# Holding back the chains of small operations between the Gram matrix and the first gradient of an image

## The chip, the cores and the metric

The kernel runs on one core of one Trainium2 chip, in one launch. The metric is the device time of that launch in microseconds (us). The kernel before took 2804.1 us, the median of three runs (2804.09, 2804.1 and 2806.65).

## What is computed

A batch of 16 images with 64 channels of 128 x 128 points goes through four residual layers. Every layer first normalizes groups of two channels (`_gn`), and adds its result to its input:

```python
x = x + _L0_conv_ref(_gn(x), L0_conv_conv_w)   # Gram matrix over the points, times x, then a 1x1 convolution
x = x + _L1_conv_ref(_gn(x))                   # |Sobel x| + |Sobel y| of each channel
x = x + _L2_conv_ref(_gn(x), L2_conv_W, L2_conv_b)      # shifted 3x3 convolution
x = x + _L3_conv_ref(_gn(x), L3_conv_w_bin, L3_conv_w1x1, ...)  # 3x3, 1x1, batch norm over all images, clip
```

The first layer is linear in the image once the image's Gram matrix (64 x 64) and its channel sums are known:

```python
gram = jnp.einsum('bcn,bdn->bcd', xf, xf) / N
y = jnp.einsum('bcd,bdn->bcn', gram, xf)
out = jnp.einsum('oc,bchw->bohw', conv_w, y)
```

So the kernel needs the Gram sums of an image, makes from them one matrix per image that carries the whole first layer and the mean and deviation that the second layer's normalization needs, and applies it while it computes the gradients. The batch norm at the end needs sums over all the images.

## The kernel before

**Stages and steps.** Four stages work on different images at once: `Gram` (Gram sums on the matmul engine), `Front` (first layer as a matmul, then the Sobel gradients), `Layer2` and `Layer3`. An image has NS = 8 tiles, and one pass of the main loop over `step` moves each stage by one tile. `starts` says that image b reaches tile 0 of `Front` at step 15 + 8b, of `Layer2` at 25 + 8b and of `Layer3` at 35 + 8b. A step has four quarters, q = 0 to 3. All instructions are recorded through `InOrder`, so every engine executes them in the order in which the loop writes them; an engine whose next instruction waits does nothing else.

In what follows a step is named by the tile i that `Front` works on, i = (step - 15) mod 8. Eight steps make a period, in which one image passes each stage.

**Gram.** `pace` tells at which step an image's Gram work begins, and whether it goes at single or double speed. Images 1 to 6 go at double speed, four steps apart, and end at steps 16, 20, 24, 28, 32 and 36. Images 7 to 15 go at single speed and end at steps 47, 55, ... 111. At single speed the 128 matmuls per image come in blocks of 44, 42 and 42: in quarters 0 and 2 of a step with i = 7 and in quarter 0 of the step with i = 0 after it. At double speed all lie in one step. `pg` is their sum in PSUM; its pool `ps_g` has one buffer, which `pe` of `Front` uses too.

**The chain.** When the last block is issued, `gram_chain(b, pg)` is put into the list `chains`. It is a generator: `tick()` runs at the end of each quarter and lets each chain do one more piece, up to its next `yield`. One chain has 44 operations on VectorE, 19 matmuls (into the one PSUM tile `bank`) and two square roots on ScalarE, in 19 pieces, over four and a half steps. The pieces, by the names of what they write:

1. `gs`, the copy of `pg` out of PSUM
2. the matmuls `gd`; then `g`, `st`, `junk0`; the matmuls `pm`; then `me`, `nv`, `var` and the root `sd`
3. `r` (four operations) and `vv` (five); the matmuls `pr`; then `rw`; the matmul `pc`; then `cs`, `rc`
4. the matmuls `pq`; then `r2`, `wbd`, `ad`, `abd`; the matmuls `pd`; then `pp`, `av`; the matmuls `pk`
5. `bias`, `st1`, `t1`; the matmuls `pm`; then `me`, `nv`, `var`, `sd`; then `r` and `co1`

At the end `abd` (the matrix) and `co1` (the coefficients) are put into `lead[b]`. `Front` takes them at quarter 1 of its step -2, that is step 13 + 8b. The chain issues no DMA and nothing on GpSimd. The chains of the other two normalizations (`coefficients`) are in the same list.

**The order around it.** Within a quarter the loop writes `Layer3`, `Layer2`, `Front`, then `Gram`, then `tick()`. The instructions of `Front` that matter are: on VectorE `u<-xh`, the first of a step, with `e<-xh`; four operations on `u` and `e` in quarter 1; one each in quarters 2 and 3. On ScalarE, in quarter 2, two absolute values of `u` and `e` and then `xh<-po`, which empties the matmul's result `po` into `xh`. On the matmul engine `po<-x,abd` in quarters 1 and 3. `po` has one PSUM buffer, so the matmul in quarter 3 waits until ScalarE has emptied the one of quarter 1, and ScalarE has ahead of that the absolute values that wait for VectorE. `Layer2` issues `one<-v,wi` as its first matmul in quarter 2, and in the same tile of work `y` of `Layer3` is the first large VectorE operation of the quarter. `Layer2` also has GpSimd compute `edges` and correct `v`, for which VectorE's last `d<-v` of a step waits.

Of the kernel before, what the change touches and what calls it, by code (L numbers as in the profile page):

```python
# [10 lines left out]
F32 = mybir.dt.float32  # L11
# [4 lines left out]
B, C, H, W = 16, 64, 128, 128  # L16
P = 128
# [4 lines left out]
NS = HH // R  # L22
EARLY = 3
# [85 lines left out]
def tile_kernel(ctx: ExitStack, tc: tile.TileContext, x, cw_h, w2_t, b2, wbin_t, w1_t, b1, gamma, beta, consts, out):  # L109
# [11 lines left out]
    def k(name):  # L121
        return kc[:, AT[name][0]:AT[name][1]]
# [39 lines left out]
    stp = ctx.enter_context(tc.tile_pool(name="stp", bufs=2))  # L162
# [6 lines left out]
    def sv(name, n=1):  # L169
        return small.tile([P, n], F32, tag=name, name=name)  # L170
# [6 lines left out]
    def small_product(dst, wt, src):  # L177

        for o in (1 - last[0], last[0]):
            pe.matmul(dst[cols(o)], wt[:, cols(o)], src, start=True, stop=True)  # L180
        last[0] = o
# [5 lines left out]
    def sm(n, rows=P):  # L187
        if n > 8:
            return bank[0:rows, P:P + n]
        turn[0] = (turn[0] + 1) % 16  # L190
        return bank[0:rows, 8 * turn[0]:8 * turn[0] + n]
# [55 lines left out]
        nc.gpsimd.memset(twins[name], 0.0)  # L247


    chains = []  # L250

    def tick():
        for c in list(chains):
            if next(c, chains) is chains:
                chains.remove(c)
# [44 lines left out]

    def gram_chain(b, pg):

        gs = stp.tile([P, C + 1], F32, tag="gs", name=f"gs_{b}", bufs=1)
        dve.tensor_copy(gs, pg)
        if b > 1:
            yield
        gd = sm(C + 1)
        small_product(gd, k("same"), gs)
        yield
        g = stp.tile([P, C + 1], F32, tag="g", name=f"g_{b}", bufs=1)  # L310
        dve.tensor_scalar_mul(g, gd, 1.0 / HW)
        mu = g[:, C:C + 1]
        st = sv("st0", 2)
        dve.tensor_copy(st[:, 0:1], mu)
        junk0 = stp.tile([P, C], F32, tag="junk0", name=f"junk0_{b}", bufs=1)
        dve.scalar_tensor_tensor(
            junk0, g[:, 0:C], 1.0, k("Id"), op0=ALU.mult, op1=ALU.mult, accum_out=st[:, 1:2]
        )
        if b > 1:
            yield  # L320
        pm = sm(2)
        small_product(pm, k("gavg"), st)
        yield
        r, mean = yield from rstd(pm, GN_EPS)

        vv = sv("vv", 5)
        dve.tensor_scalar_mul(vv[:, 0:1], mu, -1.0)
        dve.tensor_sub(vv[:, 1:2], mu, mean)
        dve.tensor_copy(vv[:, 2:3], mu)
        dve.tensor_sub(vv[:, 3:4], mu, mean)  # L330
        dve.tensor_scalar_mul(vv[:, 4:5], mean, -1.0)
        if b > 1:
            yield
        pr = sm(2 * P, rows=2)
        pe.matmul(pr[:, 0:P], vv[:, 0:2], k("hsame"), start=True, stop=True)
        pe.matmul(pr[:, P:2 * P], vv[:, 2:4], k("hsame"), start=True, stop=True)
        yield
        rw = stp.tile([2, 2 * P], F32, tag="rw", name=f"rw_{b}", bufs=1)
        dve.tensor_copy(rw, pr)
        if b > 1:  # L340
            yield
        pc = sm(C)
        pe.matmul(pc, rw[:, 0:P], rw[:, P:P + C], start=True, stop=True)
        yield

        cs = stp.tile([P, 2, C], F32, tag="cs", name=f"cs_{b}", bufs=1)
        for s in range(2):
            dve.tensor_add(cs[:, s, :], pc, g[:, 0:C])
        rc = stp.tile([P, C], F32, tag="rc", name=f"rc_{b}", bufs=1)
        dve.tensor_scalar(rc, cwh, r, 0.5, op0=ALU.mult, op1=ALU.mult)  # L350
        csf = cs.rearrange("p s c -> p (s c)")
        if b > 1:
            yield
        pq = sm(C)
        small_product(pq, csf, rc)
        yield
        r2 = sv("r2")
        dve.tensor_mul(r2, r, r)
        for s in range(2):
            rows = slice(s * C, (s + 1) * C)  # L360
            dve.tensor_scalar_mul(wbd[rows, rows], pq[rows], r2[rows])
        ad = stp.tile([P, C], F32, tag="ad", name=f"ad_{b}", bufs=1)
        dve.scalar_tensor_tensor(ad, pq, r2, k("Id"), op0=ALU.mult, op1=ALU.add)
        abd = stp.tile([P, P], F32, tag="abd", name=f"abd_{b}", bufs=EARLY + 3)
        dve.tensor_add(abd, wbd, k("I"))
        if b > 1:
            yield
        pd = sm(C + 3)
        small_product(pd[:, 0:C], csf, ad)
        small_product(pd[:, C:C + 2], abd, vv[:, 2:4])  # L370
        small_product(pd[:, C + 2:C + 3], wbd, vv[:, 4:5])
        yield
        pp = stp.tile([P, 2, C], F32, tag="pp", name=f"pp_{b}", bufs=1)
        for s in range(2):
            dve.tensor_mul(pp[:, s, :], pd[:, 0:C], ad)
        av = sv("av", 3)
        dve.tensor_copy(av, pd[:, C:C + 3])
        if b > 1:
            yield
        pk = sm(1)  # L380
        small_product(pk, pp.rearrange("p s c -> p (s c)"), k("q"))
        yield
        bias = sv("bias")
        dve.tensor_copy(bias, av[:, 2:3])
        st1 = sv("st1", 2)
        dve.tensor_add(st1[:, 0:1], av[:, 0:1], bias)
        t = sv("t1")
        dve.scalar_tensor_tensor(t, av[:, 1:2], av[:, 1:2], pk, op0=ALU.mult, op1=ALU.subtract)
        dve.scalar_tensor_tensor(
            st1[:, 1:2], st1[:, 0:1], st1[:, 0:1], t, op0=ALU.mult, op1=ALU.subtract  # L390
        )
        if b > 1:
            yield
        pm = sm(2)
        small_product(pm, k("gavg"), st1)
        yield
        r, mean = yield from rstd(pm, GN_EPS)

        co = stp.tile([P, 4], F32, tag="co1", name=f"co1_{b}", bufs=EARLY + 3)
        dve.tensor_copy(co[:, 0:1], r)  # L400
        dve.tensor_sub(co[:, 1:2], bias, mean)
        dve.tensor_mul(co[:, 1:2], co[:, 1:2], r)
        dve.reciprocal(co[:, 2:3], r)
        dve.tensor_copy(co[:, 3:4], mean)
        lead[b] = abd, co

    class Gram:
# [5 lines left out]
        def at(self, i, q):  # L413
# [29 lines left out]
            if n == 6:  # L443
                chains.append(gram_chain(b, self.pg))
# [416 lines left out]
    starts = ((Layer3, 35), (Layer2, 25), (Front, 15))  # L861
    live = {}

    def run(stage, b, i, q):
        if 0 <= b < B and stage.first <= i <= stage.last:
            if (stage, b) not in live:
                live[stage, b] = stage(b)
            live[stage, b].at(i, q)
# [27 lines left out]
    def slices(t, n):  # L896
        room.extend(t[:, j * N:(j + 1) * N] for j in range(n))
# [11 lines left out]
            fetched[0] += 1  # L909

    for step in range(steps):
        for q in range(4):
            for b in range(B):

                i = step - starts[2][1] - NS * b
                if 0 <= i < NS and q in (0, 2):
                    live[Front, b].sobel(i, f"first of {q}")
                if q == 3:
                    run(Layer2, b, step - starts[1][1] - NS * b, "first of 3")
            for stage, at in starts:  # L920
                for b in range(B):
                    run(stage, b, step - at - NS * b, q)
            if q == 3:
                for b in range(B):
                    run(Layer2, b, step - starts[1][1] - NS * b, "last of 3")
            for b in range(B):
                at, n = pace[b]
                for m in range(n):
                    v = 4 * n * (step - at) + n * q + m
                    run(Gram, b, v // 4, v % 4)  # L930
            tick()

            if step == last_one - NS and q == 0:
                slices(xw.rearrange("p w c t -> p (w c t)"), 8)
                slices(xh.rearrange("p a j w -> p (a j w)"), 3)
                rest(xin, "x", [R, W], 2)
                rest(xin, "xr", [C // 8, W], 3)
                rest(work, "u", [R + 1, W + 2], 2)
                rest(work, "e", [R, W + 2], 1)
            if step == last_one and q == 0:  # L940
                rest(ring, "v2", [(R + 1) * W + 2], 3)
                for t in (diffs["d2"], twins["d2"]):
                    slices(t.rearrange("p n j w -> p (n j w)"), 1)
            if step >= last_one and q == 2:

                n = 3 if step == last_one else 1 if step < last_one + NS - 2 else 0
                rest(ring, "x3", [2, CP, W], NS + 2, n)

            if step >= last_one - NS and q == 3 and len(room) > 1:
                fetch()  # L950
# [82 lines left out]
```

## Time and profile before

| what | us |
|---|---|
| median of the three runs | 2804.1 |
| the profiled execution, its own time | 2800.37 |
| its span, from first to last instruction | 2798.6 |
| matmul engine (PE) busy | 2222.1 |
| VectorE (DVE) busy | 2201.4 |
| ScalarE (ACT) busy | 2120.1 |
| GpSimd (POOL) busy | 859.5 |
| the last matmuls, those of the batch norm's sums | 2349.13 |

Times inside a profile count from the start of its span. The part from 2349 us on is the last pass, which reads two arrays, adds them and writes the output; the change does not touch it. Before it, the main loop goes through three stretches: up to about 329 us (step 34) the pipeline fills; from there to about 1760 us (step 118) all stages work, Gram sums among them; from there to step 155 there are no Gram sums left to make.

A view of windows gives, for each stretch of time, how long each engine was busy in it and (in brackets) with how many instructions. The busy time of the matmul engine has modelled ends and says little on whether it waited; the starts of its instructions in the timeline do.

### The profile page before, as it was taken

To read this page: it belongs to the slowest core of one execution; us is meant where nothing else is said; L and a number is where in the kernel's file an instruction comes from. 1 tells how busy PE (TensorE), PEld (TensorE's weight loads), DVE (VectorE), ACT (ScalarE), POOL (GpSimd) and SP (SyncE) were. 2 spreads that over 40 slices of the span, in tenths; PEclk is the share of its full clock that TensorE was granted. 3 is DMA by queue.
4 is the path that set the end of the run, shared out by engine and by line. 5 is a ranking of instruction groups with operands and counts; after the bars stand their busy time and mean duration, and the time that the engine had idled before them with its cause. 6 is when DMAs were issued, how large, how long until landed. Compare 5 with 4: busy or idle time off the path is not lost. (4 is left out here: it accounts for less than half of the span.)

```text
span 2798.6 us, 46299 instructions
## 1 busy us (share of the span) xinstructions
PE 2222.1 (79%) x14772; PEld 1088.8 (39%) x14772; DVE 2201.4 (79%) x3758; ACT 2120.1 (76%) x3171; POOL 859.5 (31%) x1326
## 2 busy tenths in 40 slices
PE   4568899999999999999999999999999995000000
PEld 2323444444444545353534353566666641000000
DVE  3999999898989898989898989999997435333332
ACT  4667779888888888888888888998997667333332
POOL 1035433343434343434343434444444310000000
PEclk7679999999999999999999999999999998555555
DMA  6789878888888888888888777888877767999999
GB/s 168 196 221 233 237 198 237 218 232 212 230 215 221 222 220 219 222 216 227 221 219 227 214 184 197 209 204 214 209 207 187 218 192 273 420 420 420 420 420 387
DMA packets 688880, 685.95 MB, mean 245 GB/s; under 512 B 61744, under 2 KB 590144, under 8 KB 688640
## 3 DMA queue, kind: packets, MB, share of 16 engines
q1 hardware_dynamic: 662656, 614.42, 73.9%
q0 software_dynamic: 24576, 68.12, 10.0%
q8 instruction: 119, 1.95, 0.3%
q14 instruction: 121, 0.99, 0.1%
q10 hardware_dynamic: 1408, 0.46, 0.1%
HBM read 346.23 MB, written 268.44 MB: 220 GB/s over the span
## 5 line engine op out<-in xcount | busy, mean ns | idle before, releaser
L73 PE MATMUL two<-d,w 128*64 128x508 f32 (+2 forms) x2560 | 898.2, 586 | 0.0
L73 PE MATMUL two<-d,wi 128*64 128x508 f32 (+3 forms) x1536 | 626.6, 576 | 0.0
L73 POOL DMA_DIRECT2D qd<-d x512 | 269.8, 529 | 882.2 <-issue 330.0
L73 PE MATMUL two<-qd,pk 128*64 128x512 f32 (+1 forms) x1024 | 518.5, 587 | 1.6 <-DMA qd<-d 1.1
L73 POOL TENSOR_SCALAR edges<-v,co 64x8 f32<-64x8 f32 x512 | 335.2, 655 | 352.5 <-ACT v L73 244.4
L73 PE MATMUL po<-x,abd 128*64 128x512 f32 x1024 | 386.2, 631 | 60.4 <-ACT xh L73 60.4
L73 PEld LDWEIGHTS two<-d,w 128*64 128x64 f32 x2560 | 297.9, 136 | 288.7 <-issue 221.2
L73 PE MATMUL one<-v,w 128*64 128x508 f32 (+2 forms) x1600 | 409.0, 578 | 0.0
L73 PE MATMUL one<-v,wi 128*64 128x508 f32 (+3 forms) x1536 | 407.4, 590 | 0.0
L73 DVE TENSOR_TENSOR d<-v 128x512 f32<-128x512 f32 (+1 forms) x512 | 346.1, 679 | 44.4 <-POOL v L73 17.1
L73 ACT COPY qd<-d 64x512 f32<-64x512 f32 x512 | 315.2, 616 | 21.0 <-DVE d L73 14.5
L73 ACT ACTIVATE xh<-po,co 128x128 f32<-128x128 f32 (+1 forms) x480 | 275.3, 621 | 51.0 <-PE po L73 48.7
L73 DVE SCALAR_TENSOR_TENSOR e<-e 128x1032 f32<-128x1032 f32 (+1 forms) x256 | 313.2, 1223 | 0.0
L73 DVE SCALAR_TENSOR_TENSOR y<-two,c 128x1024 f32<-128x1024 f32 x128 | 156.1, 1219 | 125.6 <-ACT v L73 72.4
L73 PEld LDWEIGHTS two<-d,wi 128*64 128x64 f32 x1536 | 196.1, 135 | 143.2 <-issue 107.7
L73 POOL TENSOR_SCALAR v<-v,kc 128x9 f32<-128x9 f32 x256 | 238.4, 944 | 11.9
L73 ACT ACTIVATE v<-x,co 128x512 f32<-128x512 f32 (+2 forms) x368 | 234.9, 704 | 0.0
L73 PEld LDWEIGHTS one<-v,w 128*64 128x64 f32 x1600 | 163.3, 137 | 177.4 <-issue 130.0
L73 PEld LDWEIGHTS one<-v,wi 128*64 128x64 f32 x1536 | 156.0, 138 | 162.6 <-issue 126.4
L73 ACT ACTIVATE u<-u 128x1024 f32<-128x1024 f32 x128 | 135.4, 1058 | 90.3 <-DVE u L73 89.9
L73 DVE SCALAR_TENSOR_TENSOR u<-xh 128x1170 f32<-128x1170 f32 x128 | 175.7, 1372 | 12.2 <-ACT xh L73 9.8
L73 PEld LDWEIGHTS po<-x,abd 128*64 128x64 f32 x1024 | 111.0, 140 | 175.4 <-ACT xh L73 92.3
(154 smaller groups left out, 3442.4 us busy)
## 6 DMA issues: line engine op xcount, KB each, us to landing
xr<-in_x SPq DMA_DIRECT2D x128, 512.0 KB, 6.7
x<-in_x SPq DMA_DIRECT2D x256, 256.0 KB, 4.0
x_d<-u SPq DMA_DIRECT2D x512, 128.0 KB, 3.6
y_d<-y SPq DMA_DIRECT2D x512, 128.0 KB, 4.0
x_d<-x SPq DMA_DIRECT2D x496, 128.0 KB, 2.5
qd<-d POOLq DMA_DIRECT2D x256, 130.0 KB, 3.0
qd<-d POOLq DMA_DIRECT2D x256, 129.8 KB, 3.6
v<-x_d SPq DMA_DIRECT2D x448, 72.1 KB, 3.0
```

Of the source, the lines that this page charges most:

```text
L73: return self.tc.keep_in_program_order(call(*args, **kwargs))
```

## The change

`gs` is copied as before, one tick after the Gram matmuls. The chain then yields until the step counter has reached 15 + 8b - 9, that is, until nine steps ahead of tile 0 of the image's `Front`, a step with i = 7. It goes on from there with the same pieces in the same order. `gs` gets five buffers in place of one. `abd` gets three in place of six, and `co1` four in place of six. Images 0 and 1 get their Gram sums later than that step and don't wait.

```diff
+    now = [0]
     chains = []
...
     def gram_chain(b, pg):
 
-        gs = stp.tile([P, C + 1], F32, tag="gs", name=f"gs_{b}", bufs=1)
+        gs = stp.tile([P, C + 1], F32, tag="gs", name=f"gs_{b}", bufs=EARLY + 2)
         dve.tensor_copy(gs, pg)
         if b > 1:
             yield
+
+        while now[0] < starts[2][1] + NS * b - 9:
+            yield
         gd = sm(C + 1)
...
-        abd = stp.tile([P, P], F32, tag="abd", name=f"abd_{b}", bufs=EARLY + 3)
+        abd = stp.tile([P, P], F32, tag="abd", name=f"abd_{b}", bufs=3)
...
-        co = stp.tile([P, 4], F32, tag="co1", name=f"co1_{b}", bufs=EARLY + 3)
+        co = stp.tile([P, 4], F32, tag="co1", name=f"co1_{b}", bufs=4)
...
     for step in range(steps):
+        now[0] = step
         for q in range(4):
```

The pieces after `gs` move as follows:

| image | step of the copy, before and after | steps of the other pieces before | after |
|---|---|---|---|
| 1 | 16 | 17 to 21 | the same |
| 2 | 20 | 21 to 25 | 22 to 26 |
| 3 | 24 | 25 to 29 | 30 to 34 |
| 4 | 28 | 29 to 33 | 38 to 42 |
| 5 | 32 | 33 to 37 | 46 to 50 |
| 6 | 36 | 37 to 41 | 54 to 58 |
| 7 | 47 | 47 to 52 | 62 to 66 |
| ... | | | |
| 14 | 103 | 103 to 108 | 118 to 122 |
| 15 | 111 | 111 to 116 | 126 to 130 |

## The prediction

> **What bounds the kernel now.** I read the page first, then busy times step by step (windows cut where VectorE starts `u<-xh`), then timelines. The page, with busy tenths in 40 slices of 70 us:
>
> ```profile
> PE 2222.1 (79%) x14772; PEld 1088.8 (39%) x14772; DVE 2201.4 (79%) x3758; ACT 2120.1 (76%) x3171; POOL 859.5 (31%) x1326
> ...
> PE   4568899999999999999999999999999995000000
> ...
> DVE  3999999898989898989898989999997435333332
> ```
>
> Two engines are near full, and VectorE fills first. The windows of one period in the middle (i = 7, 0, 1, ... 6; columns: length, then busy time of PE, weight loads, DVE, ACT, POOL with counts), and of one period after the last Gram sums:
>
> ```profile
> 923.37:939.34 15.97, 15.97 (x175) 8.44 (x173) 14.65 (x20) 15.69 (x25) 4.45 (x10) 1.00 0.99 242
> 939.34:961.47 22.13, 22.13 (x233) 12.12 (x231) 16.35 (x35) 15.50 (x26) 4.96 (x12) 1.00 0.72 193
> 961.47:977.97 16.50, 16.50 (x125) 9.49 (x123) 16.15 (x37) 15.95 (x26) 5.79 (x11) 1.00 0.92 235
> 977.97:995.71 17.74, 17.74 (x89) 6.55 (x87) 16.94 (x31) 16.29 (x26) 8.50 (x11) 1.00 0.88 236
> 995.71:1013.28 17.57, 17.57 (x98) 6.29 (x96) 17.09 (x36) 15.17 (x24) 4.68 (x9) 1.00 0.80 216
> 1013.28:1029.33 16.05, 16.05 (x84) 6.79 (x82) 15.64 (x28) 14.96 (x24) 6.16 (x12) 1.00 0.84 234
> 1029.33:1045.24 15.91, 14.89 (x69) 8.06 (x67) 15.59 (x28) 13.72 (x23) 8.42 (x11) 1.00 0.82 208
> ...
> sum 136.77, PE 135.75 PEld 62.70 DVE 126.96 ACT 122.05 POOL 50.38; mean PE 16.97 PEld 7.84 DVE 15.87 ACT 15.26 POOL 6.30
> ```
>
> ```profile
> 1901.03:1915.54 14.51, 14.51 (x98) 9.86 (x96) 14.37 (x20) 12.42 (x20) 6.63 (x8) 1.00 0.83 222
> ...
> sum 124.15, PE 124.15 PEld 79.95 DVE 120.59 ACT 113.39 POOL 58.31; mean PE 15.52 PEld 9.99 DVE 15.07 ACT 14.17 POOL 7.29
> ```
>
> In the middle VectorE has 9.8 us to spare per period, 7.1 of them in i = 7 and 0, where the Gram blocks hold up PE. In i = 1 to 5, where the chain is, VectorE is full and PE catches up with it, until PE has to wait in i = 5 (timeline of PE):
>
> ```profile
> 904.35 1.01 PE L73 MATMUL two<-d,wi 128*64 128x508 f32 x2
> 906.37 1.08 PE L73 MATMUL po<-x,abd 128*64 128x512 f32 x4 [1.01 <-ACT xh L73]
> ```
>
> That is the loop over VectorE's `u`, ScalarE's absolute values and `xh`, and PE's `po`. Starts 1.60 us apart where 0.43 is the spacing of such matmuls: 1.2 us lost. The PE timeline has no other such gap in a period, only about 0.3 us in small ones: 1.5 us per period lost, the rest is PE's own work. VectorE's waits in i = 0:
>
> ```profile
> 943.82 0.38 DVE L73 TENSOR_TENSOR two<-two,edges 128x8 f32<-128x8 f32 x2 [1.96 <-PE two L73]
> ...
> 954.23 1.22 DVE L73 SCALAR_TENSOR_TENSOR y<-two,c 128x1024 f32<-128x1024 f32 x1 [3.44 <-ACT junk L73]
> ```
>
> The second is really for PE: the last matmul of its `two` starts at 953.55 and takes 0.59. The reader is to see that 5.4 us of VectorE in i = 0 are free. While the pipeline fills, VectorE bounds (steps 25 to 34):
>
> ```profile
> sum 154.42, PE 127.26 PEld 55.97 DVE 143.96 ACT 107.89 POOL 82.33; mean PE 12.73 PEld 5.60 DVE 14.40 ACT 10.79 POOL 8.23
> ```
>
> [...]
>
> **The change, part by part.** Nothing is removed: 16 chains stay, with all operations, and no DMA, SyncE or GpSimd instruction is in them. Order on the engines changes, and 14 chains move. One chain on VectorE, start to start in the period shown: `g` to `junk0` 0.47, `me` to `var` 0.54, `r` and `vv` 1.03, `rw` 0.34, `cs` and `rc` 0.42, `r2` to `abd` 1.28, `pp` and `av` 0.35, `bias` to `st1` 0.78, `me` to `var` 0.52, `r` to `co1` 1.28: 7.0 us. On PE: the time from one step's first `one<-v,wi` to the next one's is 15.6, 17.0, 16.1, 15.9, 15.7 us with a chain (i = 0 to 4) and 15.4, 15.9, 15.5, 15.4, 15.4 without; less 0.3 of waits, 2.4 us.
>
> *Filling (to step 34).* By the table of steps, pieces leave steps 21 to 34 worth 10.4 us of VectorE: chain 4 (7.0), chain 5 up to `rw` and about 1 net of chain 2 moved later. Not all comes back: in steps 27 to 29, with no chain left, VectorE's last `d` would come at 11 to 12 us into the step, while GpSimd's correction of `v` ends at 12.4 to 13.3 now. I take off 4 us for that, and 1 for waiting longer on the Gram block ahead of `gs` in step 28 (0.96 us already). Gain 5 us; bounds 2 and 9.
>
> *PE's work in the full part.* Chains 6 to 15 and 0.6 of chain 5 lie after step 34 now; then chains 4 to 15 do. 1.4 more at 2.4: a loss of 3.4 us, bounds 2 and 5.
>
> *Nine periods with Gram blocks (chains 5 to 13, in place of 7 to 15).* Pieces now fall on i = 7 (1.01 us), 0 (1.37), 1 (1.70), 2 (1.13), 3 (1.80). The first 2.0 are free in VectorE's waits. There `var` waits for `pm`, which stands behind the second Gram block: PE gets there about 1.8 us after VectorE, and VectorE stands still, with the next step's `u<-xh` behind it. The 5.4 us of i = 0 cover that too; if not, that is the third rival. The rest I follow with one number, D: the start of PE's first `one<-v,wi` in a step less the start of VectorE's `u<-xh` in it. It grows by PE's time for the step and shrinks by VectorE's. Now, by the timelines, D is 8.3, 8.8, 7.2, 5.5, 5.1 at i = 1 to 5 (18.76 less 13.28 at i = 4), and in the last periods without chains 7.8 to 8.1, 9.2, 8.3, 7.4, 8.2. `po` waits once D falls under a floor, read from `xh`'s end after `u<-xh`: about 5.7 at i = 4 and 5, and 7.5 at i = 3 with a piece of 0.52 ahead of it. At i = 1, D becomes 8.3 - 0.3 (`rw`) + 1.2 (`pr`, `pc`, `pq` are on PE there by then) = 9.2. Then 9.2 + 16.4 - 16.2 = 9.4; + 15.6 - 17.5 = 7.5, just at its floor; + 15.4 - 18.1 = 4.8 at i = 4, 0.9 under its floor; after that D recovers. Lost 0.9 per period in place of 1.5: gain 0.6 times 9, 5.5 us. An error of 1 us in D is 1 us per period: bounds from a gain of 13 to a loss of 3 within one model.
>
> *The end (chains 14 and 15).* They now run where no Gram block gives VectorE a rest. D starts at about 7.9 at i = 7; with PE's and VectorE's times of that stretch and the pieces added it goes 8.7, 6.8, 7.0, 5.1, so PE loses 2.4 at i = 3 and 0.9 at i = 4: 3.3 per chain, 6.6 us, bounds 3 and 9. Before, PE waits 1.3 us for `qd` once at 1742 us, with D down from the last chain; half of it goes: 0.7.
>
> *Buffers.* Five `gs` hold three waiting sums at most (images 4 to 6 at step 36), `abd` and `co1` are in use for two images at a time. No wait; nothing. `lead[b]` is ready at step 10 + 8b and taken at 13 + 8b: no wait of `Front`.
>
> Sum: -5 + 3.4 - 5.5 + 6.6 - 0.7 = -1.2 us. Against the profiled execution (2800.37 us; span 2798.6 and 1.8 around it) that is 2799; its own time lies 3.7 under the median shown, 2804.1, to which I apply the difference and get 2803.
>
> **Rivals.** (1) *It cancels* (forecast): what filling and the Gram steps give, the end takes. 2797 to 2809.
>
> (2) *Faster.* The free time in i = 7 and 0 ends PE's waits altogether: nine times 1.5 is 13.5; filling gives 8, the end costs 4: -8 + 3.4 - 13.5 + 4 - 0.7 = -15, 2789. For it: VectorE's 7.1 us there are over three times the pieces' 2.4. Against: the other 4.6 us fall on three steps in place of 6.2 on five, and one, i = 3, already carries the small operations of `Layer3`'s coefficients.
>
> (3) *Slower.* Place: i = 3 and 4 in every period. If D at i = 1 is not 9.2 but at the 7 of the end stretch, because the wait for `pm` is not covered, PE loses 3.3 per period as there: 1.8 more than now, nine times 16. With the other terms, -5 + 3.4 + 16 + 6.6 - 0.7 = +20, 2824. It decides from D under 8.6 at i = 1, where 1.5 is lost as now. For it: i = 3 gets 1.80 us on top of a full step. Against: in i = 0 it is PE that is late, by 14.8 in D.
>
> (4) *It doesn't do what it says* for images 0 and 1, by the table; for the others the order of instructions shows the move.
>
> **How the numbers follow.** Within 0.2%, 5.6 us, is what a measurement can't tell from no change. Cancels 0.40, faster 0.27, slower 0.33, which includes couplings of the three full engines that one number D doesn't follow. The single terms' bounds together (about 3 to 9 each, of different sign) give 2793 to 2812 around the forecast alone; 2788 to 2819 takes in the faster case and the lower part of the slower one.
>
> **What would show it.** Right: steps 21 to 34 shorter by about 5 us in all; in the middle, a period of 136.2 against 136.8, VectorE's busy time in i = 7 and 0 up by 2.4 at the same lengths, the wait on `po` at i = 4 and not 5; periods from 1745 us on longer by 3 plus PE's 2.4. Wrong: i = 0 longer than 22.1 by a microsecond or more, `po` waiting over 2 us at i = 3, or no wait at all.

## The result: slower by 0.6%, and the profile after

| | before | after |
|---|---|---|
| median, us | 2804.1 | 2820.74 |
| the profiled execution, its own time | 2800.37 | 2819.42 |
| its span | 2798.6 | 2817.6 |

The ratio is 1.0058, with a 95% interval of 1.0043 to 1.0073. The forecast was 2803, its range 2788 to 2819. The page of the changed kernel shows little (busy time with its share and instructions, then busy tenths in 40 slices of the span):

```profile
PE 2235.1 (79%) x14772; PEld 1021.4 (36%) x14772; DVE 2202.8 (78%) x3758; ACT 2121.7 (75%) x3171; POOL 832.1 (30%) x1326
...
PE   3567899999999999999999999999999995000000
...
DVE  3998989898989898989898989999997435333332
```

The instructions are as many as before, and VectorE's busy time grew by 1.4 us. So for VectorE nearly all of the 19.05 us by which the span grew are waits. The windows of the middle period that answers to the one shown of before (shown are i = 7, 0, 2, 3 and the sum; columns: length, then busy time of PE, weight loads, DVE, ACT, POOL with counts, then PE's granted clock, the DMA engines' busy share and GB/s):

```profile
927.83:947.16 19.33, 19.33 (x244) 11.10 (x242) 15.68 (x27) 16.35 (x27) 5.11 (x12) 1.00 0.98 232
947.16:968.07 20.91, 20.91 (x174) 9.11 (x172) 17.60 (x45) 16.32 (x26) 5.05 (x10) 1.00 0.70 183
...
984.26:1002.99 18.73, 18.73 (x111) 10.65 (x108) 17.15 (x34) 16.10 (x26) 7.54 (x12) 1.00 0.85 236
1002.99:1020.82 17.83, 17.33 (x80) 7.36 (x78) 17.27 (x39) 15.12 (x25) 4.20 (x8) 1.00 0.81 219
...
sum 137.46, PE 136.76 PEld 60.52 DVE 127.18 ACT 122.52 POOL 49.62; mean PE 17.10 PEld 7.56 DVE 15.90 ACT 15.31 POOL 6.20
```

The period is 0.7 us longer than the one shown of before, not 0.6 shorter (over the nine periods it is 0.4 on average). Look at i = 2, which begins at 984.26: 18.73 us long with 17.15 us of VectorE's work in it. In before VectorE had 0.8 us without work in this step; here it has 1.6. The view that finds the cause sums up what VectorE waited for over the whole kernel (us in total, times, the longest). Before:

```profile
DVE me L73 <- PE bank L73: 0.9, 2, 0.5
```

After:

```profile
DVE me L73 <- PE bank L73: 37.0, 24, 3.5
```

`me` is the copy of a small product's result out of PSUM. It waited twice before, and 24 times now. Two of the 24 are the old ones; nine are in i = 7, about 1.97 us each, where the prediction had one of about 1.8 and called it covered. The other thirteen are all in i = 2, from step 33 to step 129, and nobody expected them. One of them, in the timelines of VectorE and then of PE, in i = 2 of the period above:

```profile
998.21 0.21 DVE L73 SCALAR_TENSOR_TENSOR t<-av,bank 128x1 f32<-128x1 f32 x1
...
1002.33 0.16 DVE L73 COPY me<-bank 128x2 f32<-128x2 f32 x1 [1.24 <-PE bank L73]
```

```profile
998.48 0.28 PE L73 MATMUL bank<-s,kc 128*64 128x2 f32 x4
...
1001.22 0.23 PE L73 MATMUL bank<-st,kc 128*64 128x2 f32 x2
...
1002.06 0.23 PE L73 MATMUL bank<-st,kc 128*64 128x2 f32 x2
```

Two lists of small operations meet here. `t` and `bank<-st` (the second `pm`) belong to the Gram chain. `bank<-s` and this `me` belong to the coefficients of the third normalization, the one that `Layer2` ends with. `me` reads what `bank<-s` wrote at 998.48, yet it starts only after the chain's last `bank<-st`, at 1002.06 and 3.6 us later, of which it needs nothing. And in the stretch without Gram blocks, PE's timeline and VectorE's:

```profile
1816.63 0.28 PE L73 MATMUL bank<-s,kc 128*64 128x2 f32 x4 [1.75 <-DVE t L73]
```

```profile
1816.37 0.21 DVE L73 SCALAR_TENSOR_TENSOR t<-av,bank 128x1 f32<-128x1 f32 x1
...
1820.48 0.16 DVE L73 COPY me<-bank 128x2 f32<-128x2 f32 x1 [1.24 <-PE bank L73]
```

Here PE stands 1.75 us and starts nothing else, before a matmul for which `t` gives nothing either; `s`, which it does read, was ready at 1813.2. What they share is a place. All small products of the chains are written into one PSUM bank, the narrow ones at columns that take turns:

```python
    bank = ps_sm.tile([P, 512], F32, name="bank")
    ...
    def sm(n, rows=P):
        if n > 8:
            return bank[0:rows, P:P + n]
        turn[0] = (turn[0] + 1) % 16
        return bank[0:rows, 8 * turn[0]:8 * turn[0] + n]
```

`t` reads other columns than `bank<-s` writes, and `bank<-s` waits for it all the same. The trace shows the two waits, 1.24 us of VectorE and 1.75 us of PE; by what rule they are ordered it doesn't show. The prediction counted on no wait of this kind.

So in these two waits a read and a product within `bank` keep the order in which the program writes them down, though their columns differ. In quarter 2 of i = 2 the changed program has the chain's `bias` to `t`, then the coefficients' `bank<-s`. In quarter 3 it has the chain's `bank<-st`, then the coefficients' `me`. They are out of step: in each quarter one list's VectorE piece stands beside the other's product, and whoever is behind pays. `me` has to wait for a product written down just ahead of it, with no quarter of lead. In the kernel before both had their products in quarter 2 (`pc`, which is `bank<-rw`, and `bank<-s`) and their VectorE pieces in quarter 3 (`cs` and `me`), and nobody waits (PE, then VectorE, in i = 2):

```profile
991.99 0.43 PE L73 MATMUL bank<-rw 2*128 2x64 f32 x2
992.35 0.28 PE L73 MATMUL bank<-s,kc 128*64 128x2 f32 x4
```

```profile
994.64 0.35 DVE L73 TENSOR_TENSOR cs<-bank,g 128x64 f32<-128x64 f32 x2
...
995.06 0.15 DVE L73 COPY me<-bank 128x2 f32<-128x2 f32 x1
```

Where the spans differ, from the times at which VectorE starts the steps (differences to the profile of before, us; the column e1 is the first experiment below):

| stretch | predicted | after | e1 |
|---|---|---|---|
| up to step 15 | 0 | +1.2 | +1.6 |
| steps 15 to 34 | -5 | +2.8 | -0.5 |
| steps 34 to 46 | -1.4 | -0.7 | -2.3 |
| steps 46 to 118, nine periods with Gram blocks | -5.5 | +4.0 | -5.1 |
| steps 118 to 134, chains 14 and 15 | +10.7 | +13.2 | +10.9 |
| from there on | 0 | -1.5 | -1.2 |
| sum | -1.2 | +19.0 | +3.4 |

(The PE term of the prediction is laid out here by its chains: two more after step 118, 0.6 fewer in steps 34 to 46; the -0.7 is in the end. The profiled execution of before lies 3.7 us under its median, so a column that sums to +3.4 is about level with the medians of before. The first two rows differ from execution to execution: over steps 15 to 34 the profiles of four kernels with the same order of instructions there, before, e2, e4 and e7, take 251.8 to 258.6 us. In the other rows before and e2 differ by 0.4 us at most.) While the pipeline fills, the same meeting is in step 33, and the wait is longer there (PE, then VectorE):

```profile
308.68 0.28 PE L73 MATMUL bank<-s,kc 128*64 128x2 f32 x4 [1.97 <-DVE t L73]
```

```profile
314.23 0.16 DVE L73 COPY me<-bank 128x2 f32<-128x2 f32 x1 [3.54 <-PE bank L73]
```

The windows from the start of `bank<-s` to that of `me`, in step 33 and in step 73 of the middle, show what is different:

```profile
308.68:314.23 5.55, 5.51 (x22) 1.87 (x22) 2.01 (x4) 1.91 (x3) 1.08 (x2) 0.69 1.01 249
998.48:1002.33 3.85, 3.85 (x27) 1.69 (x28) 2.61 (x6) 2.58 (x4) 0.94 (x2) 1.00 0.59 161
```

PE's granted clock was 0.69 in the one (0.50 from 310 to 313 us) and 1.00 in the other, and 5.55 times 0.69 is 3.83, about the length of the other. So by this estimate 1.7 us of the 3.54 come from the lower clock. The other 0.6 by which the wait is longer than 1.24 come from VectorE, which is at `me` that much sooner. The clock fell just after PE had stood 1.97 us for `t`; that the standing was the reason isn't shown.

### The profile page after: what moved, and what is told of

Read it like the earlier page. It is cut to its first block, busy times and chain, and to the rows that moved or that the text cites. A ratio compares the mean times of both kernels' runs of the same rounds, so it can differ in the third digit from the quotient of the medians.

```text
span 2817.6 us, 46286 instructions
## 1 busy us (share of the span) xinstructions
PE 2235.1 (79%) x14772; PEld 1021.4 (36%) x14772; DVE 2202.8 (78%) x3758; ACT 2121.7 (75%) x3171; POOL 832.1 (30%) x1326
## 5 line engine op out<-in xcount | busy, mean ns | idle before, releaser
L73 PE MATMUL two<-d,w 128*64 128x508 f32 (+2 forms) x2560 | 869.3, 587 | 0.0
L73 PE MATMUL two<-d,wi 128*64 128x508 f32 (+3 forms) x1536 | 608.4, 579 | 0.0
L73 PEld LDWEIGHTS two<-d,w 128*64 128x64 f32 x2560 | 281.1, 136 | 311.9 <-issue 258.3
L73 PE MATMUL po<-x,abd 128*64 128x512 f32 x1024 | 340.7, 632 | 64.8 <-ACT xh L73 64.0
L73 DVE TENSOR_TENSOR d<-v 128x512 f32<-128x512 f32 (+1 forms) x512 | 346.9, 680 | 47.4 <-issue 16.4
L73 PE MATMUL one<-v,w 128*64 128x508 f32 (+2 forms) x1600 | 383.8, 579 | 0.0
L73 PE MATMUL one<-v,wi 128*64 128x508 f32 (+3 forms) x1536 | 369.5, 587 | 0.0
L73 POOL TENSOR_SCALAR v<-v,kc 128x9 f32<-128x9 f32 x256 | 220.2, 873 | 11.9
L73 PEld LDWEIGHTS one<-v,w 128*64 128x64 f32 x1600 | 138.5, 136 | 183.9 <-issue 149.9
L73 PEld LDWEIGHTS one<-v,wi 128*64 128x64 f32 x1536 | 137.4, 137 | 164.2 <-issue 135.8
L73 ACT ACTIVATE v<-v,co 128x1154 f32<-128x1154 f32 x128 | 172.0, 1344 | 15.6 <-DMA v<-x_d 8.1
```

Of the source, the lines that this page charges most:

```text
L73: return self.tc.keep_in_program_order(call(*args, **kwargs))
```

## The experiments

Theory 1 says that the meeting in one bank is the loss. Theory 2, its rival, says that the place is: the chain's 7 us of VectorE lie where there is no rest, and a wait there takes what would be lost anyway. Every kernel here computes the whole result.

### e1: another bank for one of the two

```diff
-    def coefficients(st, put, back=None):
+    def coefficients(st, put, back=None, place=None):
...
-        pm = sm(2)
+        pm = sm(2) if place is None else place()
         small_product(pm, k("gmean"), s2)
...
-                    chains.append(coefficients(self.st, lambda co: coefs3.update({b: co})))
+                    chains.append(coefficients(
+                        self.st, lambda co: coefs3.update({b: co}),
+                        place=lambda: ps_g.tile([P, CP, W], F32, tag="g", name=f"ps3_{b}")[:, 0, 0:2],
+                    ))
```

> The changed kernel, with one thing different: the matmul of the sums for the third normalization (Layer2's coefficients, in the step with i = 2) writes into the PSUM bank that the Gram sums use, which is free then, and not into the bank of the chain's small products. Same instructions, same order. Theory 1 (the shared bank): in i = 2 the chain and the coefficients take turns in one bank, so PE's product waits for VectorE's `t1`, and VectorE's `me` waits for PE's `pm`; this costs the 1.24 us of VectorE seen in every i = 2, and PE's 1.9 us twice after 1745 us. Then these waits are gone, D at i = 3 goes from 6.2 to above 7, the period falls from 137.5 to about 136.5, step 33 gives back 3, and the whole is 10 to 18 us faster than the changed kernel: 2803 to 2811. Theory 2 (the place): what costs is where the chain's 7.0 us of VectorE lie (no rest after i = 0, and none at all for images 14 and 15); the meeting only takes time that would be lost anyway. Then 2818 to 2823.

Measured: 2803.8 us, ratio to before 0.9992 (0.9984 to 1.0000). Theory 2 is out as the reason for the loss. All that the change lost is back, and none of its instructions was moved on its engine. PE's and VectorE's timelines in i = 2:

```profile
990.56 0.22 PE L73 MATMUL ps<-s,kc 128*64 128x2 f32 x2
991.24 0.22 PE L73 MATMUL ps<-s,kc 128*64 128x2 f32 x2
```

```profile
991.04 0.21 DVE L73 SCALAR_TENSOR_TENSOR t<-av,bank 128x1 f32<-128x1 f32 x1
...
993.83 0.16 DVE L73 COPY me<-ps 128x2 f32<-128x2 f32 x1
```

The product no longer waits for `t` (the first two matmuls start before it), and `me` has no wait. The windows of i = 2 and the period:

```profile
977.08:994.49 17.41, 17.41 (x108) 11.52 (x105) 17.06 (x34) 16.07 (x26) 6.77 (x11) 1.00 0.88 234
...
sum 136.10, PE 135.97 PEld 63.54 DVE 127.11 ACT 122.56 POOL 49.73; mean PE 17.00 PEld 7.94 DVE 15.89 ACT 15.32 POOL 6.22
```

i = 2 is shorter by 1.32 us, the period shown by 1.36, and the nine periods by 9.1 in all, 1.0 each. What VectorE still waits for at `me` are the nine waits in i = 7 and the two old ones:

```profile
DVE me L73 <- PE bank L73: 18.7, 11, 2.0
```

18.3 us in 13 waits are gone, and the span is 15.6 us shorter. The new place is another bank and also another tile of the program. Whether the wait hangs on the bank or on the tile `bank` as a whole is not separated by any run here.

### e2: the same other bank in the kernel before

The edit is that of e1, made in the kernel before.

> The kernel before, with the same other bank for the third normalization's sums as in the run beside it. It is the control. There the chain and the coefficients have their products in the same quarter and their VectorE pieces in the same quarter, so neither theory expects a wait to go: 2801 to 2807, that is, no change that can be told.

Measured: 2806.4 us, ratio 1.0002 (0.9994 to 1.0011). As expected: another bank by itself was worth nothing here, it is the meeting that it takes away.

### e3: the bank stays shared, the chains start a quarter later

```diff
         while now[0] < starts[2][1] + NS * b - 9:
             yield
+        if b > 1:
+            yield
```

> The changed kernel with every held chain starting one quarter later, so that in i = 2 its products and those of the coefficients fall into the same quarter; the bank stays shared. Theory 1 (the shared bank): the waits in i = 2 go here too, 2803 to 2813; a new meeting with the second normalization's coefficients, in the quarter 2 of i = 0, lies in time that VectorE has free. Theory 2 (the place): a quarter of a step moves little, 2817 to 2824.

Measured: 2832.99 us, ratio 1.0100 (1.0086 to 1.0113). Both theories missed. The wait in i = 2 is gone as theory 1 had it. But there is another (VectorE, in i = 0):

```profile
969.66 0.16 DVE L73 COPY me<-bank 128x2 f32<-128x2 f32 x1 [2.73 <-PE bank L73]
```

```profile
969.03 0.60 PE L73 MATMUL bank<-kc,vv 128*2 128x128 f32 x4
```

This `me` belongs to the second normalization's coefficients, whose product was done at 964.7; it waited for the chain's `pr`, four matmuls at 969.03, written down just ahead of it. The free time of i = 0 did not hold it: that time is the wait of `y`, which ended at 963.90, ahead of this one. The next `u<-xh` starts late, D at i = 1 is 6.1 in place of 8.8, and PE, with less in reserve, stands in i = 3 (timeline of PE):

```profile
1023.25 1.08 PE L73 MATMUL po<-x,abd 128*64 128x512 f32 x4 [1.21 <-ACT xh L73]
```

So a shift by one quarter moved the meeting from one pair of lists to another. That this is the reason was still a reading of the trace; e5 tests it.

### e4: only images 14 and 15 held back

```diff
-        while now[0] < starts[2][1] + NS * b - 9:
+        while b > 13 and now[0] < starts[2][1] + NS * b - 9:
             yield
```

`abd` and `co1` have the six buffers of before.

> Only images 14 and 15 are held back as in the change; all others go at once as before, with the buffers of before for the matrix and the coefficients. Both theories: nothing differs up to step 103, and the end of the change comes alone. From the marks of the two profiles, the end has lost 12.75 us between step 118 and step 135, against the chains 14 and 15 that the steps 103 to 116 get rid of, about 2 times 1.0 to 3 us. If the loss adds up stretch by stretch: 2809 to 2815. If it is much less than that, the end loses because of what the middle left behind.

Measured: 2807.73 us, ratio 1.0006 (0.9998 to 1.0015), so less than expected. By the steps' times against before, steps 102 to 118, now without chains, are 10.7 us shorter, and steps 118 to 134 are 13.6 longer. The end does lose as much as in the changed kernel, but most of it is refunded: a chain that leaves a middle period saves 5.4 us, not 1 to 3. The 13.2 us of the table are no net loss. They are mostly the price of two chains, which the kernel before paid in the middle. The 2.9 us left over hold the two meetings, which e4 has as well (1.24 us of `me` in steps 121 and 129); without them e1 loses 2.3 us less there.

### e5: all three lists in step, one bank

The edit is that of e3, and one `yield` more after the second normalization's sums (`back` is given for that one only):

```diff
         dve.tensor_reduce(s2, st, axis=AX.X, op=ALU.add)
         yield
+        if back is not None:
+            yield
```

> The changed kernel with every held chain one quarter later, as in the third run, and the second normalization's coefficients (which are put into the list in quarter 0 of the step with i = 0) one quarter later too: their product then lies in the quarter of the chain's `pr` and their `me` in that of `rw`. The bank stays shared by all. Theory 1 (the shared bank): the third run was slow because its quarter moved the meeting from i = 2 into i = 0, where VectorE's `me` stood 2.73 us for the chain's product; with nobody out of step the wait is gone in both places, D at i = 1 comes back from 6.1 to above 8, and the time is that of the run with the other bank, 2800 to 2810. Theory 2 (the place): a quarter later is a worse place for the chain's pieces as such (PE's wait on `po` of 1.8 us at i = 3), and the coefficients are nothing to it: 2826 to 2834.

Measured: 2806.83 us, ratio 1.0006 (0.9998 to 1.0014). One `yield` in a list of 14 small operations on VectorE takes back 26 us of e3, with the bank shared by all and the chain in the place that was so slow. VectorE's waits, then the same period's sum:

```profile
DVE me L73 <- PE bank L73: 0.9, 2, 0.5
```

```profile
sum 136.10, PE 135.63 PEld 64.31 DVE 127.19 ACT 121.86 POOL 51.31; mean PE 16.95 PEld 8.04 DVE 15.90 ACT 15.23 POOL 6.41
```

`me` waits as in the kernel before, and the period shown is as long as that of e1. e1 still has the 1.97 us in i = 7 and e5 has not; over the nine periods e5 is 1.9 us shorter, so that wait costs some 0.2 us each time, if it is the whole difference.

### e6: the meeting made in the kernel before

```diff
         dve.tensor_copy(gs, pg)
         if b > 1:
             yield
+            yield
```

> The kernel before with one thing different: each chain waits one more quarter after `gs`. In i = 2 its `rw` then lies in the quarter of the coefficients' product, and its product `pc` in front of their `me`: the meeting of the changed kernel, made in the kernel before. Theory 1 (the shared bank): VectorE waits about 1 to 1.5 us for PE in i = 2 of each of the nine periods, D at i = 3 falls from 7.2 to about 6, and the time is 2812 to 2822. Theory 2 (the place): a quarter later alone changes nothing that counts, 2802 to 2809.

Measured: 2835.27 us, ratio 1.0107 (1.0093 to 1.0121). The direction is theory 1's; the loss of 30 us is twice what it expected. In the middle it was right: VectorE waits in i = 2,

```profile
1022.74 0.16 DVE L73 COPY me<-bank 128x2 f32<-128x2 f32 x1 [1.56 <-PE bank L73]
```

and steps 38 to 118 lose 12.6 us. The rest comes while the pipeline fills (20.1 us against the profile of before at step 38; the other profiles with that order of instructions are up to 9.3 behind it there), where the Gram work of images 1 to 6 ends every four steps, so that chains lie at other places against the coefficients. In step 31 both sides of the meeting stand (PE, then VectorE):

```profile
280.26 0.38 PE L73 MATMUL bank<-s,kc 128*64 128x2 f32 x4 [6.46 <-DVE cs L73]
280.58 5.22 PE L73 MATMUL one<-v,wi 128*64 128x512 f32 x12
```

```profile
288.50 0.16 DVE L73 COPY me<-bank 128x2 f32<-128x2 f32 x1 [6.94 <-PE two L73]
```

PE waits for VectorE to read in `cs`, and with PE late by that, VectorE's next read waits for PE. The step is 6.8 us longer than before. Here too PE was slow after it had stood: the twelve `one<-v,wi` took 5.22 us, where twelve of the same shape in the changed kernel (at 1025.98 us, at a granted clock of 1.00) took 2.74.

### e7: e1 with images 2 to 6 not held back

```diff
-        while now[0] < starts[2][1] + NS * b - 9:
+        while b > 6 and now[0] < starts[2][1] + NS * b - 9:
             yield
```

The bank is that of e1, the buffers of `abd` and `co1` are those of before.

> The kernel of the first run (changed kernel, other bank for the third normalization's sums), with images 2 to 6 not held back, and the buffers of before for the matrix and the coefficients. It undoes the part of the change that empties the filling stretch and puts 1.4 more chains into the full one. If the filling gains 5 us from being rid of the chains, as the prediction had it, and a chain costs the full stretch 2.4 us of PE and 1 of waits: 2803.8 + 5 - 5 = 2804, the same as the first run. If the filling gains nothing from it (its length is set by transfers and GpSimd), and a chain in the full stretch costs 5.7 us (what the fourth run's profile saves per period in steps 103 to 118): 2803.8 - 8 = 2796, faster than both kernels.

Measured: 2800.28 us, ratio 0.9983 (0.9977 to 0.9990): faster than both kernels, by 0.17% against before. It lies between the two expectations. Its step 38 comes 5.8 us later after step 15 than in e1, which has the sign and about the size of the filling's gain as the prediction had it, though two single profiles can differ by that much there. The three periods from there to step 62 are 9.8 us shorter. They hold most of chain 6 in place of chains 4, 5 and 6, so that is over 4 us for each chain that they are rid of. So a chain is dearer in the full stretch than while the pipeline fills.

## Why the prediction was wrong

**The step that failed** is the one that follows D through i = 2: "Then 9.2 + 16.4 - 16.2 = 9.4; + 15.6 - 17.5 = 7.5, just at its floor". The 17.5 for VectorE's step i = 2 was made of the pieces' durations and knew of no wait: what two lists do to each other in one bank was put at nothing, without being named. The step took 18.73, because of the 1.24 us for which `me` waits. D, the start of PE's first `one<-v,wi` less that of VectorE's `u<-xh`, read from the timelines:

| D at | i = 1 | i = 2 | i = 3 | i = 4 |
|---|---|---|---|---|
| predicted | 9.2 | 9.4 | 7.5 | 4.8 |
| after | 8.8 | 9.0 | 6.2 | 5.2 |
| e1, other bank | 8.8 | 9.0 | 7.2 | 5.2 |

Up to i = 2 D is 0.4 off. At i = 3 it falls 1.3 under the prediction and below the floor of 7.5, and PE loses 0.7 us ahead of `po` in i = 3 and some 0.5 in i = 4, by the spacing of its matmuls. With the meeting gone, i = 2 lasts 17.41 where 17.5 was predicted, the period shown 136.10 where 136.2 was, and PE loses 0.1 in i = 3 and 0.5 in i = 4, where the forecast had 0.9 in i = 4. So the mechanism that D follows was right, and the missing wait is what broke it.

**Point by point.**

- *Filling* (-5): single profiles can't decide it, by the spread given with the table. The medians help, as the rest of the span repeats well. The changed kernel's median is 16.6 us above that of before, and from step 34 on its profile lost 15.0, which leaves a loss of some 1.6 for the filling: no gain, with 3.75 us lost to the meeting in step 33 (20.38 us, 16.63 in e1). The median of e1 is 1.8 under that of before, and from step 34 on its profile lost 2.3, which leaves a gain of some 4. Both are estimates from these figures.
- *PE's work* (+3.4): only a part of a chain's price. With the 1.5 us of waits in a period, the prediction had 3.9 us for a chain in the middle; e4 shows 5.4 us saved per chain that leaves a period there. What makes up the rest isn't shown.
- *Nine periods* (-5.5): +4.0 in the changed kernel, -5.1 without the meeting. That a piece costs nothing where VectorE would wait anyway was the author's assumption; what was measured is that the wait of 1.97 us in i = 7 cost some 0.2 us (e5 against e1, if that is the whole difference).
- *The end* (+6.6 with two chains' PE time): 10.7 in all, measured 13.2, and 10.9 without the meeting; but in the changed kernel PE's longest wait lies a step earlier than thought, 1.75 us in i = 2 for `t`, and in both D stops at 6.2 to 6.4 at i = 3 where 5.1 was predicted, so the sum came out better than its parts.
- *Buffers* (nothing): e1 keeps the new buffer numbers and has the whole loss back, so they aren't the reason. The order within the bank belonged under that heading and wasn't there: the shared resource was `bank`, not `gs`, `abd` or `co1`.
- *The signs*: none of the three that were to show the forecast wrong came (i = 0 lasts 20.91 us, `po` waits under 2 us at i = 3, and it does wait). Of those that were to show it right, one failed even in e1, where the period came out: i = 7 and 0 did not keep their lengths but are 2.1 us longer together, and i = 4 and 5 are 2.4 shorter.

**The rivals.** The third (slower, 2824) came nearest in its time by luck, for its reason was wrong. The wait for `pm` in i = 7 came, 1.97 us where about 1.8 was expected, and was covered as the forecast had it: D at i = 1 is 8.8, above the 8.6 under which that rival would have begun, and e5 without the wait has e1's period. The forecast's sum describes e1, the change without the meeting: -1.2 predicted, and 2803.8 against 2805.56 us of before measured beside it, -1.8.

What stays open: whether VectorE's reads and PE's writes of one bank could be freed of this order within the bank (as two tiles, say) wasn't tried. The loss of a single meeting is known by stretch only, from the two columns of the table: 9.1 us for the nine in steps 46 to 118, 2.3 for the two at the end, 1.5 for the one in step 41; VectorE waits 1.24 us in each.

## What to carry to other kernels

When lists of small operations take turns through one PSUM bank, look at which quarter each has its product and its read in: here a read that was written down right behind another list's product waited for that product, though it had other columns: 1.24 us in i = 2 of each middle period, 2.73 in e3's i = 0. Moving one list by a step or a quarter moves these meetings, so check every other list that uses the bank at the new place, and bring them in step (e5, 26 us faster than e3) or give one another bank (e1, 17 us faster than the changed kernel). And price a piece of work in a stretch where two engines are full by what a period without it saves (5.4 us here), not by its busy time on one engine (7.0 and 2.4).

## What the runs showed that wasn't expected

- One `yield` in a list of small operations decided over 26 us, about 1% (e3 against e5), with no instruction added or taken away.
- The waits differ by place: 1.24 to 1.56 us in the middle's i = 2, 2.73 in e3's i = 0, 3.54 in step 33, and 6.94 in step 31 of e6. In the last two PE had just stood (1.97 and 6.46 us) and was slow then: in step 33 its granted clock was 0.50 for 3 us, which by the estimate above is 1.7 us of the wait, and in step 31 twelve matmuls took 5.22 us that take 2.74 in the middle.
- A wait of 1.97 us in every i = 7 cost little (e5, without it, is 0.2 us shorter per period), and one of 1.24 us in i = 2, ahead of the step in which D has no reserve, cost 1.0 on average.
